# Ten small GpSimd transfers in place of four for each of four x loads: which engine writes which SBUF rows at a time

## The chip, the cores and the metric

The kernel runs on one core of one Trainium2 chip. The metric is the device time of one execution in microseconds, the median of several runs. Before the change it is 1314.01 us (three runs, 1313.97 to 1316.09). Next to the compute engines (TensorE, here PE; VectorE, here DVE; ScalarE, here ACT; GpSimd, here POOL; SyncE, here SP) the core has sixteen DMA engines, numbered 0 to 15, that move data between HBM and SBUF. "Engine 4" and the like always means a DMA engine below.

## The reference

The input is `r_inputs` of shape (4096, 32, 64), 32 fields of 64 float32 numbers for each of 4096 batch rows. For every pair of fields i < j, 496 pairs in all, there is a 64 x 64 weight matrix. What is computed:

```python
i_idx, j_idx = np.triu_indices(32, k=1)
vi = inputs[:, i_idx, :]
vj = inputs[:, j_idx, :]
vdotw = jnp.einsum('bpd,pde->bpe', vi, W)
inter = vdotw * vj
return inter.reshape(B, -1)
```

So each pair's result is a product of a 64-vector with the pair's matrix, multiplied element by element with the other field. The output has 4096 x 496 x 64 float32 numbers, 520 MB, and the inputs are 42 MB: the work is mostly writing.

## The kernel before

**Tiles.** The batch is cut into eight chunks of 512 rows (`BANK`). Two fields make a field pair and fill the 128 partitions, so one chunk of x is 16 tiles of 128 x 512; all 16 lie in one SBUF tensor `x` that is not doubled. All weights stay in SBUF (`w`). A chunk is worked through in 128 steps: for each group of four field pairs (`GROUP`), first a step for the pairs among themselves (L208, L228), then steps of one pair against another (L218, L236). PE writes the products into a ring of eight PSUM banks, and DVE multiplies them with x and writes the result into a slot.

**Slots and stores.** Three slots of 20, 18 and 18 blocks form a ring. When a slot is full, SP issues one store of 4.6 or 5.1 MB (L180), and DVE may write the slot again when that store has landed. Stores are on SP's DMA queue (q1 in the profile).

**x loads.** The next chunk's x comes in two loads: groups 0 and 1 when the current chunk is done with group 1 (L249 to L251), groups 2 and 3 at the chunk's end. Most are one transfer of 128 rows of 16 KB from ACT (L140; q10), eight rows on each DMA engine. The first load of chunks 1, 3, 5 and 7 (`LIGHT_CHUNKS`) is different: it leaves engine 4 out, and goes from GpSimd's queue (L99; q0).

**How engines are chosen.** [...] `from_engine(e)` (L101) issues a "nudge", a transfer of a few bytes on k engines into an otherwise unused tile, so that the next transfer starts at engine e. `load_beside` (L113) then issues, before the change, two transfers for a load: the last eight rows, four each on two engines (from `PAIRS_FROM`: 7 and 8, 15 and 0, 1 and 2, 7 and 8), and rows 0 to 119, eight each on engines 5 to 15 and 0 to 3. With the nudges these are four transfers per load. `kernel` (L273 to L281) lays the rows out in HBM so that each engine reads one stretch, with a pad of 16 numbers between stretches.

**Order.** Instructions stay in program order on each engine. GpSimd's x transfers wait for the PE and DVE instructions that read the old x (an old x is read by PE as moving operand and by DVE as second factor). [...]

Of the kernel before, what the change touches and what calls it, by code (L numbers as in the profile page):

```python
# [8 lines left out]
F32 = mybir.dt.float32  # L9
ALU = mybir.AluOpType  # L10

P = 128
# [7 lines left out]
DMA_ENGINES = 16  # L20
LIGHT = 4
LIGHT_CHUNKS = [1, 3, 5, 7]
PAIRS_FROM = [7, 15, 1, 7]
HEAD = P // DMA_ENGINES
REST = HEAD // 2
PAD = 16


# [33 lines left out]
def is_light(load):  # L62

    return load[1] == 0 and load[0] in LIGHT_CHUNKS


def load_size(load):

    pads = (DMA_ENGINES + 1) * PAD if is_light(load) else 0
    return P * (load[2] - load[1]) * GROUP * BANK + pads  # L70


# [1 line left out]
def pair_bilinear_kernel(  # L74
# [16 lines left out]
    const = ctx.enter_context(tc.tile_pool(name="const", bufs=1))  # L91
    psum = ctx.enter_context(tc.tile_pool(name="ps", bufs=1, space=bass.MemoryType.PSUM))

    nudges = [const.tile([DMA_ENGINES, 16], F32, tag=f"nudge{i}", name=f"nudge{i}") for i in range(2)]
    cursor = 0

    def from_pool(out, in_):

        tc.keep_in_program_order(nc.gpsimd.dma_start(out=out, in_=in_))  # L99

    def from_engine(e):  # L101

        nonlocal cursor
        k = (e - cursor) % DMA_ENGINES
        if k:
            nudge = nudges[e == LIGHT + 1]
            from_pool(
                nudge[:k].rearrange("p (h c) -> p h c", h=2)[:, :, :4],
                x[: k * 8].rearrange("(p h c) -> p h c", p=k, h=2),
            )  # L110
        cursor = e

    def load_beside(at, xt, n_row, lap):  # L113

        nonlocal cursor
        most = DMA_ENGINES - 1
        for e, k, rows, p in (
            (PAIRS_FROM[lap], 2, REST, most * HEAD),
            (LIGHT + 1, most, HEAD, 0),
        ):  # L120
            from_engine(e)
            n = rows * n_row
            lines = x[at : at + k * (n + PAD)].rearrange("(k c) -> k c", k=k)
            from_pool(xt[p : p + k * rows], lines[:, :n])
            at += k * (n + PAD)
            cursor = (e + k) % DMA_ENGINES
# [4 lines left out]
    def load_x(load):  # L131

        at = sum(load_size(before) for before in loads[: loads.index(load)])
        c, g0, g1 = load
        n = (g1 - g0) * GROUP * BANK
        xt = xbuf[:, g0 * GROUP * BANK : g0 * GROUP * BANK + n]
        if is_light(load):
            load_beside(at, xt, n, LIGHT_CHUNKS.index(c))
        else:
            nc.scalar.dma_start(out=xt, in_=x[at : at + P * n].rearrange("(p c) -> p c", p=P))  # L140

    for load in loads:
        if load[0] == 0:
            load_x(load)
# [42 lines left out]
    for c in range(NC):  # L187
        todo = list(enumerate(steps))
        while todo:
            if made == base + room:  # L190
                turn += 1
                base, room = made, SLOTS[turn % len(SLOTS)]
                tag = f"slot{turn % len(SLOTS)}"
                osb = ring.tile([P, room * BANK], F32, tag=tag, name=tag)
            (s, (p, q)), rest = todo[0], todo[1:]
            n = 1
# [28 lines left out]
            if q is None:  # L225
                for h in range(2):
                    rows = slice(h * D, (h + 1) * D)
# [21 lines left out]
            for load in loads:  # L249
                if last and load[0] == c + 1 and load[2] == p // GROUP + 1:  # L250
                    load_x(load)  # L251
# [58 lines left out]
```

## Time and profile before

| What | Value |
|---|---|
| median of the runs | 1314.01 us |
| profiled execution, its own time | 1313.63 us |
| its span | 1311.8 us |
| moved by DMA | 562.39 MB, 429 GB/s on the mean |
| PE, DVE, POOL busy | 81%, 88%, 1% |
| DVE waits for a slot's store | 77.9 us in 48 waits |
| stores, issue to landing (4.6 MB) | 23.6 us, 68 of them |
| x load from ACT, issue to landing | 20.9 us |
| large part of an x load from GpSimd, issue to landing | 31.3 us |

The span is the time from the first to the last instruction on the core; 1.8 us of the profiled execution lie around it. "Issue to landing" runs from the instruction that issues a transfer to the event that tells of its end, and so includes the time that its packets stand in a queue. The share of a DMA queue is the time of its packets as a part of sixteen engines' span.

### The profile page before, as it was taken

The numbers are of one execution on the slowest core, as the hardware profiler recorded it, in microseconds if no ns is written. First come the engines' busy times: TensorE is split into PE (matmuls) and PEld (weight loads), VectorE is DVE, ScalarE is ACT, GpSimd is POOL, SyncE is SP. The second block draws the span as 40 slices with busy tenths as digits, with TensorE's granted clock in tenths as the row PEclk, the third lists the DMA queues.
The fourth block names the chain that finished last, engine by engine and source line by source line (L and its number), as shares of the span: only waits on it lengthen the run. The fifth ranks groups of instructions, "written<-read, shape, count | busy, mean of one in ns | idle before, by whom it ended". The sixth has DMA issues, their size and how long they took to land.

```text
span 1311.8 us, 9391 instructions
## 1 busy us (share of the span) xinstructions
PE 1058.4 (81%) x4096; PEld 401.8 (31%) x4096; DVE 1153.6 (88%) x725; POOL 9.4 (1%) x20
## 2 busy tenths in 40 slices
PE   6888788988778878888788887888777798878882
PEld 2333233333323323333333332323222333233230
DVE  6998789998899879998889998899888998889893
POOL 0000000000000000000000000000000000000000
PEclk9999899998999989999999999899999999999996
DMA  9999999999999999999999999999999999999998
GB/s 390 429 438 432 422 436 431 432 432 433 432 434 429 434 430 432 431 433 430 436 426 437 434 425 423 434 434 435 431 428 435 428 432 429 427 431 437 434 430 363
DMA packets 19625, 562.39 MB, mean 429 GB/s; under 512 B 2688, under 2 KB 2688, under 8 KB 2816
## 3 DMA queue, kind: packets, MB, share of 16 engines
q1 hardware_dynamic: 16560, 528.23, 93.6%
q10 hardware_dynamic: 1872, 25.17, 4.5%
q0 software_dynamic: 1152, 8.39, 1.6%
q8 instruction: 32, 0.52, 0.1%
q14 instruction: 9, 0.07, 0.0%
HBM read 41.68 MB, written 520.09 MB: 428 GB/s over the span
## 4 chain that ended last, share of the span: by engine, by line
DMA 52%; DVE 38%; PE 6%; issue 2%; DVEq 0%
DMA out_dram<-slot 51%; DVE slot L236 34%; PE pring L218 6%; DVE slot L228 3%; PE pring L208 1%; DMA x<-in_x_dram 1%; DVEq L236 0%; DVEq L298 0%; DVEq L228 0%
## 5 line engine op out<-in xcount | busy, mean ns | idle before, releaser
L236 DVE TENSOR_TENSOR slot<-pring,x 128x1024 f32<-128x1024 f32 (+1 forms) x661 | 1078.2, 1699 | 123.3 <-DMA out_dram<-slot 77.9
L218 PE MATMUL pring<-x,w 64*128 64x512 f32 x3840 | 996.3, 628 | 213.1 <-DVE slot L236 202.2
L218 PEld LDWEIGHTS pring<-x,w 64*128 64x128 f32 x3840 | 386.1, 192 | 824.1 <-DVE slot L236 506.3
L228 DVE TENSOR_TENSOR slot<-pring,x 64x1024 f32<-64x1024 f32 x64 | 77.9, 1217 | 13.7 <-PE pring L208 13.2
L208 PE MATMUL pring<-x,w 64*64 64x512 f32 x256 | 65.4, 631 | 16.6 <-DVE slot L236 8.7
L208 PEld LDWEIGHTS pring<-x,w 64*64 64x64 f32 x256 | 15.7, 137 | 61.3 <-DVE slot L236 28.1
L99 POOL DMA_DIRECT2D x<-in_x_dram x8 | 4.7, 588 | 1078.6 <-DVE slot L236 955.8
L99 POOL DMA_DIRECT2D nudge<-in_x_dram x8 | 4.6, 571 | 0.9 <-POOLq L294 0.9
L294 POOL MEMSET const-bfloat16-1.0<- 128x1 bf16 x1 | 0.1, 102 | 0.0
L294 POOL MEMSET const-float32-0.0<- 128x1 f32 x1 | 0.1, 99 | 0.2 <-issue 0.2
L294 POOL MEMSET const-float32-1.0<- 128x1 f32 x1 | 0.1, 99 | 0.0
L294 POOL MEMSET const-uint8-127<- 128x1 uint8 x1 | 0.1, 99 | 0.0
## 6 DMA issues: line engine op xcount, KB each, us to landing
out_dram<-slot SPq DMA_DIRECT2D x68, 4608.0 KB, 23.6
out_dram<-slot SPq DMA_DIRECT2D x35, 5120.0 KB, 22.6
x<-in_x_dram ACTq DMA_DIRECT2D x11, 2048.0 KB, 20.9
out_dram<-slot SPq DMA_DIRECT2D x4, 2560.0 KB, 21.4
x<-in_x_dram POOLq DMA_DIRECT2D x4, 1920.0 KB, 31.3
out_dram<-slot SPq DMA_DIRECT2D x2, 2048.0 KB, 22.4
w<-in_w_dram SPq DMA_DIRECT2D x1, 2816.0 KB, 30.8
x<-in_x_dram ACTq DMA_DIRECT2D x2, 1024.0 KB, 9.5
```

The lines of the kernel that those rows point to most:

```text
L99: tc.keep_in_program_order(nc.gpsimd.dma_start(out=out, in_=in_))
L208: nc.tensor.matmul(pm[o * D : (o + 1) * D, ts(k, BANK)], w_sb[m * D : (m + 1) * D, s * P + k * D : s * P + (k + 1) * D], x_of(pair, m), st ...
L218: nc.tensor.matmul(pm[:, ts(2 * i + k, BANK)], w_sb[m * D : (m + 1) * D, ts(s + i, P)], x_of(p, m), start=True, stop=True,)
L228: nc.vector.tensor_tensor(strided(osb[rows, a : a + BANK], [BANK, 2]), strided(pm[rows, :BANK], [BANK, 2]), strided(x_of(p + 1 - h, h), [2 ...
L236: nc.vector.tensor_tensor(strided(osb[:, a : a + BANK], *blocks_of), strided(pm[:, :BANK], *blocks_of), strided(x_of(q), [BANK, n], [0, 2] ...
L294: nc = bacc.Bacc("TRN2", target_bir_lowering=False, num_devices=1)
```

## The change

`load_beside` now issues six x transfers for a load, each with its first engine, its number of engines and its first row in `LIGHT_PARTS`: one row each on engines 15, 0, 1 and 2 (rows 28 to 31), two rows each on 7 and 8 (rows 60 to 63), four each on 5 to 11 (rows 0 to 27), four each on 12 to 15 and 0 to 3 (rows 64 to 95), and then four each again on both groups (rows 32 to 59 and 96 to 127). Four nudges per load keep the cursor in step, three within the load and one ahead of it, so that there are ten transfers. Between the fourth and the fifth part the cursor has to move by one engine only; that nudge has 3 x 2 x 4 elements on the SBUF side and 2 x 3 x 4 on the HBM side[...]. The nudges use four small tiles in turn. The layout of x in HBM follows. The ACT loads, the stores and all compute stay as they are.

```diff
-PAIRS_FROM = [7, 15, 1, 7]
-HEAD = P // DMA_ENGINES
-REST = HEAD // 2
+QUAD = 4
+LIGHT_PARTS = [(15, 4, 28), (7, 2, 60), (5, 7, 0), (12, 8, 64), (5, 7, 32), (12, 8, 96)]
...
     def from_engine(e):
 
-        nonlocal cursor
+        nonlocal cursor, turns
         k = (e - cursor) % DMA_ENGINES
-        if k:
-            nudge = nudges[e == LIGHT + 1]
+        nudge = nudges[turns % len(nudges)]
+        if k == 1:
+            from_pool(
+                nudge[:3].rearrange("p (h c) -> p h c", h=2)[:, :, :4],
+                x[:64].rearrange("(g r c) -> g r c", g=2, r=4)[:, :3, :4],
+            )
+        elif k:
             from_pool(
                 nudge[:k].rearrange("p (h c) -> p h c", h=2)[:, :, :4],
                 x[: k * 8].rearrange("(p h c) -> p h c", p=k, h=2),
             )
+        turns += k > 0
         cursor = e
 
-    def load_beside(at, xt, n_row, lap):
+    def load_beside(at, xt, n_row):
 
         nonlocal cursor
-        most = DMA_ENGINES - 1
-        for e, k, rows, p in (
-            (PAIRS_FROM[lap], 2, REST, most * HEAD),
-            (LIGHT + 1, most, HEAD, 0),
-        ):
+        for e, k, p in LIGHT_PARTS:
             from_engine(e)
+            rows = QUAD if k > QUAD else QUAD // k
             n = rows * n_row
             lines = x[at : at + k * (n + PAD)].rearrange("(k c) -> k c", k=k)
             from_pool(xt[p : p + k * rows], lines[:, :n])
             at += k * (n + PAD)
             cursor = (e + k) % DMA_ENGINES
```

More of the change, by code (lines that the diff above doesn't have):

```diff
@@ L67, in load_size @@
 def load_size(load):
-    pads = (DMA_ENGINES + 1) * PAD if is_light(load) else 0
+    pads = sum(k for _, k, _ in LIGHT_PARTS) * PAD if is_light(load) else 0
     return P * (load[2] - load[1]) * GROUP * BANK + pads
@@ L92, in pair_bilinear_kernel @@
     psum = ctx.enter_context(tc.tile_pool(name="ps", bufs=1, space=bass.MemoryType.PSUM))
-    nudges = [const.tile([DMA_ENGINES, 16], F32, tag=f"nudge{i}", name=f"nudge{i}") for i in range(2)]
-    cursor = 0
+    nudges = [const.tile([DMA_ENGINES, 16], F32, tag=f"nudge{i}", name=f"nudge{i}") for i in range(4)]
+    cursor = turns = 0
     def from_pool(out, in_):
@@ L137, in load_x @@
         if is_light(load):
-            load_beside(at, xt, n, LIGHT_CHUNKS.index(c))
+            load_beside(at, xt, n)
         else:
@@ L275 @@
         if is_light(load):
-            k = (DMA_ENGINES - 1) * HEAD
-            for part in (rows[k:].reshape(2, -1), rows[:k].reshape(DMA_ENGINES - 1, -1)):
+            for _, k, p in LIGHT_PARTS:
+                part = rows[p : p + (QUAD * k if k > QUAD else QUAD)].reshape(k, -1)
                 x.append(np.pad(part, ((0, 0), (0, PAD))).ravel())
```

## The prediction

> **What bounds the kernel now.** I read the strip of slices first, then the queues, the chain that ended last, the stretches around the x loads, and at last the single packets.
>
> ```profile
> PE   6888788988778878888788887888777798878882
> DVE  6998789998899879998889998899888998889893
> DMA  9999999999999999999999999999999999999998
> q1 hardware_dynamic: 16560, 528.23, 93.6%
> q10 hardware_dynamic: 1872, 25.17, 4.5%
> q0 software_dynamic: 1152, 8.39, 1.6%
> DMA 52%; DVE 38%; PE 6%; issue 2%; DVEq 0%
> ```
>
> The DMA row never falls below 9 before the tail, and the queues' shares (93.6, 4.5, 1.6) sum to 99.7% of sixteen engines: the kernel is the DMA's own time. The chain alternates stores and VectorE because the store ring holds three slots. VectorE is 88% busy, so it has room to catch up.
>
> ```profile
> 125.00:165.00 40.00, 33.02 (x120) 11.81 (x119) 33.39 (x22) 2.04 (x4) 0.91 1.00 424
> 285.00:325.00 40.00, 33.69 (x116) 12.92 (x114) 33.03 (x24) 0.00 (x0) 0.91 1.00 431
> ```
>
> These are stretches of 40 us, with GB/s last. Around the four loads from GpSimd (those I call light) I find 424, 432, 425 and 429; around the same loads from ACT 431, 432 and 433. So all that the light loads lose against plain ones is about (8+0+7+3)/432 of 40 us = 1.7 us. In the packet records a 16 KB packet takes 611 ns and a 36 KB one 1364; packets longer than their size's median add up, in the four light stretches, to 1.85 us per engine on the mean. [...]
>
> The other thing is how long a light load takes:
>
> ```profile
> x<-in_x_dram ACTq DMA_DIRECT2D x11, 2048.0 KB, 20.9
> x<-in_x_dram POOLq DMA_DIRECT2D x4, 1920.0 KB, 31.3
> 124.80 0.58 POOL L99 DMA_DIRECT2D x<-in_x_dram  x1 [122.77 <-PE pring L218]
> 125.92 0.59 POOL L99 DMA_DIRECT2D x<-in_x_dram  x1
> 167.47 1.93 PE L208 MATMUL pring<-x,w 64*64 64x512 f32 x8
> 169.94 2.46 DVE L228 TENSOR_TENSOR slot<-pring,x 64x1024 f32<-64x1024 f32 x2
> ```
>
> With eight rows on most engines both times, the GpSimd load needs 31.3 us and ACT's 20.9. From the first x issue (124.80) to the landing are 1.1 + 31.3 = 32.4 us: it is there at 157.2, and the chunk's first matmul is at 167.5, 10.3 us later. The other three land at 478.0, 797.1 and 1120.1 for matmuls at 490.5, 808.3 and 1132.2. That cover of 10 to 12 us is what I now spend.
>
> [...] an engine with a full store queue shows one GpSimd packet after each 1.364 us store packet, and a packet of 4 bytes (9 ns) costs a turn as a row of 16 KB does. [...] an engine without rows gets four-byte packets in their place. In the second load, after the transfer of four rows on two engines, the others show five small packets one turn apart, then the nudge's two. So a transfer costs every engine (rows per engine + 1) packets. Per load: 5 (two engines, four rows) + 2 (nudge) + 9 (15 engines, eight rows) + 2 (nudge) = 18; 18 x 4 x 16 = 1152, the queue's count exactly. [...]
>
> **The change, part by part.**
>
> *Rows.* Each engine's sum over four loads is unchanged: engines 7 and 8 had 12, 8, 8, 12 rows and get 10 each time; 15, 0, 1 and 2 get 9 instead of 12 once; engine 4 none. Bytes: zero.
>
> *Ports.* [...] I take half of the 1.85 us as won: -0.9 (0 to -1.85).
>
> *GpSimd's instructions.* 24 more at 0.58 us (24 x 0.58 = 13.9 us) on an engine that is 1% busy. They bring 24 x 2 completion and dummy packets and more; at some 5 ns from start to start that is 15 x 4 x 5 ns = 0.3 us of engine time.
>
> *Completion lanes.* The last x part waits until the first (one row on four engines) has landed, some 9 us after issue. Behind it on GpSimd stands only the next nudge. The engines then still have packets of earlier parts, so this costs nothing; without them it would be 3 to 4 us.
>
> *Turns.* The order up to the last x part is now 1, nudge, 2, nudge, 4, 4, nudge, 4, 4 rows per engine: 2+2+3+2+5+5+2+5+5 = 31 packets instead of 5+2+9 = 16. The mean store turn is (16 x 1.364 + 8 x 1.514)/27 = 1.257 us, since each ninth store packet is a completion of no length. Check on before: 16 x 1.257 + 12 x 0.611 + 4.1 (issue to first packet) + 1 = 32.5, seen 32.4. Fifteen more turns are 18.9 us (20.5 at 1.364; I take 19.7), less two rows of 0.61: +18.5. A light load lands 50.9 us after its first issue.
>
> *Where the stall goes.* Issues at 124.8, 445.3, 764.5 and 1087.5 land at 175.7, 496.2, 815.4 and 1138.4: 8.2, 5.7, 7.1 and 6.2 us after the matmuls that read them ran before. PE waits with all matmuls behind it; VectorE follows. PE then restarts slow: after its wait at launch the same matmuls took
>
> ```profile
> 7.93 3.68 PE L208 MATMUL pring<-x,w 64*64 64x512 f32 x8 [7.93 <-DMA x<-in_x_dram]
> 11.66 2.46 DVE L228 TENSOR_TENSOR slot<-pring,x 64x1024 f32<-64x1024 f32 x2 [11.66 <-PE pring L208]
> ```
>
> 3.68 us, not 1.93. So VectorE is late by 10.0, 7.5, 8.9 and 8.0. The next stores, issued at 181.1, 496.6, 820.1 and 1148.3 before, come at 191.1, 504.1, 829.0 and 1156.3, with packets 1.0 us later: 192.1, 505.1, 830.0, 1157.3. The store ahead of each was finished, on the mean engine, at 190.6, 500.7, 830.3 and 1156.7 (from the records; engines spread 4 to 8 us around it). Engine by engine, counting only those already empty, the mean idle is 1.5 + 4.4 + 0.5 + 0.9 = 7.3 us.
>
> *Sum:* +7.3 + 0.3 - 0.9 = +6.7 on the profiled execution of 1313.63 us (1311.8 span and 1.8 around it), which is 0.4 below the median of 1314.01. On the median: 1320.7. VectorE's 77.9 us of waiting for slots does not have to shrink for this: an engine that stood empty has lost that time.
>
> **Bounds.** Landing 2 us earlier, the same sum gives 3.1 us of idle: 1314.0 + 3.1 - 0.6 = 1316.5. Landing 2 us later, or PE slow for that much longer, nearly every engine is empty in all four places: 14.2 us, 1327.6. From there each microsecond counts four times: 3 us later, 18.2, or 1331.6.
>
> **Rivals.**
>
> *The stores in the queue cover it.* Stores land 23.6 us after issue and take about 11, so some 12 us of work is ahead of each; VectorE late by 7 to 10 leaves 2 to 5. For: in the sum above ten engines are still busy in the third place and five in the fourth. Against: after a light load the queue is at its shortest (496.6 was issued with the mean engine 4 us from empty). 1313.1 to 1316.5.
>
> *The small packets take no turns in the new order* (they merge, or go while the store queue is between packets), the load lands by 160, and only the ports remain: 1314.0 - 0.9 = 1313.1, not slower. It decides where the load lands less than 43 us after issue. Against: the spacing of one turn in the records of before.
>
> *The cursor drifts.* The nudge for one engine (3 by 2 by 4 elements against 2 by 3 by 4) moves it by another count. Then engine 4 gets 4 + 3 x 8 = 28 rows, 17 us, and ends about 13.7 us behind the last: 1334 with the stall. Against: nudges by k were exact in all four laps of before (the engine with 1396 ns store packets has no rows).
>
> *A larger stall.* Each restart also starves the slots after it: 1329 to 1345.
>
> **How the numbers follow.** Landing late with emptied queues, 1316.6 to 1329: 0.66. Covered by queued stores: 0.14. No turns: 0.07. Larger stall: 0.09. Drift: 0.04. A measurement here can tell about 0.2% (2.6 us). The range 1314 to 1331 leaves out the drift, most of the larger stall and some of the two cases without a loss. Faster by over 0.2% would need more than the ports can give: 0.03. Within: 0.19, mostly the covered case. Slower: 0.78. The likeliest's own range is 1316.6 to 1329.
>
> **What would show it.** Right: q0 with 33 x 4 x 16 = 2112 packets and unchanged 8.39 MB; the last x part of a light load landing about 50 us after the first issue; PE L208 waiting for x in four places, 5 to 15 us each; PEclk low just after; a DMA row with dents near 192, 505, 830 and 1157 and VectorE waiting less for slots. Ports right: long packets gone in the light stretches. Wrong: no wait for x (turns), waits for x with the DMA share still 1.00 (cover), or one engine's stores ending far behind (drift).

## The result, and the profile after

The changed kernel takes 1336.02 us (median of five runs, 1331.63 to 1338.23) against 1314.01 (five runs, 1311.45 to 1316.09): a ratio of 1.0163, with a 95% interval of 1.0150 to 1.0176. It is 22.0 us slower; 6.7 were forecast, and the range ended at 1331. The profiled execution takes the median's 1336.02 us, with a span of 1333.9, so 22.1 us more span than before. Of all the executions told of below one ran slow (1631.63 us, of run p2): it counts in p2's median and not in its ratio.

From the page of the changed kernel: the strip (the span in 40 equal slices), the queues, and the chain that ended last.

```profile
PEclk9999969999999987999899997999989999799996
DMA  9999989999999998999999999999999999999998
GB/s 393 435 437 424 426 372 437 423 425 427 436 425 436 425 421 380 437 423 420 431 436 427 433 423 408 395 427 434 418 432 431 433 434 423 412 392 422 439 428 383
q1 hardware_dynamic: 16560, 528.23, 92.8%
q10 hardware_dynamic: 1872, 25.17, 4.4%
q0 software_dynamic: 2112, 8.40, 1.6%
DVE 45%; DMA 41%; PE 8%; issue 4%; POOL 0%; DVEq 0%; POOLq 0%
DVE slot L238 43%; DMA out_dram<-slot 25%; DMA x<-in_x_dram 16%; PE pring L220 7%; DVE slot L230 3%; PE pring L210 1%; POOL x L98 0%; POOL nudge L98 0%; DVEq L300 0%; DVEq L238 0%; POOLq L300 0%; DVEq L230 0%
```

The rate of the kernel before, slice by slice:

```profile
GB/s 390 429 438 432 422 436 431 432 432 433 432 434 429 434 430 432 431 433 430 436 426 437 434 425 423 434 434 435 431 428 435 428 432 429 427 431 437 434 430 363
```

q0 has 2112 packets and 8.40 MB, as worked out. The rate falls to 372, 380, 395 and 392 GB/s in four slices two chunks apart, where it was 431 to 436 before, and the queues' shares now sum to 98.8% instead of 99.7%. The x loads, 1% of the chain before, are 16% of it. (Two lines were added above L208: before's L208, L218, L228 and L236 are L210, L220, L230 and L238 here.)

The chain of waits of the changed kernel, as engine, line, what it waited for, us in total, times, longest:

```profile
DVE slot L230 <- PE pring L210: 66.3, 7, 14.7
PEld pring L210 <- issue: 66.2, 73, 8.4
DVE slot L238 <- DMA out_dram<-slot: 52.6, 32, 5.0
PE pring L210 <- DMA x<-in_x_dram: 38.6, 6, 7.6
POOL x L98 <- DMA x<-in_x_dram: 18.6, 4, 4.9
```

The same waits in the kernel before:

```profile
PE pring L208 <- DMA x<-in_x_dram: 7.9, 1, 7.9
DVE slot L228 <- PE pring L208: 13.2, 2, 11.7
```

PE now waits for x at L210 in four places (six waits: one is the launch, and the fourth place has two); before, the only such wait was the one of 7.9 us at launch. DVE stands behind PE for 66.3 us there instead of 13.2, and its waits for a slot's store fall from 77.9 us to 52.6: it now often comes later than the landing that it waited for.

The first of the four places in the timeline of the changed kernel, GpSimd first and then PE and DVE (start, us, engine, line, operation, idle time ahead of it):

```profile
124.64 0.54 POOL L98 DMA_DIRECT2D x<-in_x_dram  x1 [122.63 <-DVE slot L238]
...
133.86 0.55 POOL L98 DMA_DIRECT2D x<-in_x_dram  x1 [4.62 <-DMA x<-in_x_dram]
```

```profile
169.77 1.93 PE L210 MATMUL pring<-x,w 64*64 64x512 f32 x2 [4.33 <-issue]
178.94 3.67 PE L210 MATMUL pring<-x,w 64*64 64x512 f32 x6 [7.23 <-DMA x<-in_x_dram]
```

```profile
182.65 2.48 DVE L230 TENSOR_TENSOR slot<-pring,x 64x1024 f32<-64x1024 f32 x2 [14.73 <-PE pring L210]
```

Of the eight matmuls that ran at 167.47, two start at 169.77, and the other six wait for x until 178.94, 54.3 us after the first x issue. Those six take 3.67 us, where all eight took 1.93. The same happens at 506.7, 832.3 and 1160.1, which is 53.3, 54.5 and 54.6 us after the first issue. One window of five microseconds behind each of these places (stretch, us, PE, PEld, DVE and POOL busy, PEclk, DMA share, GB/s):

```profile
190.00:195.00 5.00, 4.33 (x20) 1.84 (x19) 4.24 (x3) 0.00 (x0) 1.00 0.10 41
510.00:515.00 5.00, 5.00 (x13) 2.45 (x13) 3.67 (x3) 0.00 (x0) 0.50 0.28 120
840.00:845.00 5.00, 4.58 (x19) 2.02 (x16) 4.05 (x3) 0.00 (x0) 0.99 0.79 342
1175.00:1180.00 5.00, 4.25 (x20) 1.70 (x18) 5.00 (x5) 0.00 (x0) 1.00 0.51 220
```

DMA is down to a tenth in the first. That is the loss in plain sight: the next store is issued at 194.2 (181.1 in the kernel before), and by then every DMA engine has run dry.

The packet records give the sizes. Set one behind the other for each engine, they leave gaps of 13.8 us on the mean engine outside launch and tail (before: 0.0). Packets that take longer than the median of their size ("long packets" below) exceed it by 16.5 us per engine in all (before: 7.1). The mean engine ends 23.9 us later: 13.8 + 9.4 + 0.7. Idle engines were forecast, at 7.3 us. The 9.4 us of longer packets were not, and most of the experiments are about them.

### The profile page after: what moved, and what is told of

It reads as the page before. It is cut to its first block, busy times and chain, and to the rows that moved or that the text cites. A ratio compares the mean times of both kernels' runs of the same rounds, so it can differ in the third digit from the quotient of the medians.

```text
span 1333.9 us, 9432 instructions
## 1 busy us (share of the span) xinstructions
PE 1066.9 (80%) x4096; PEld 404.9 (30%) x4096; DVE 1151.7 (86%) x725; POOL 23.0 (2%) x44
## 3 DMA queue, kind: packets, MB, share of 16 engines
q0 software_dynamic: 2112, 8.40, 1.6%
## 4 chain that ended last, share of the span: by engine, by line
DVE 45%; DMA 41%; PE 8%; issue 4%; POOL 0%; DVEq 0%; POOLq 0%
DVE slot L238 43%; DMA out_dram<-slot 25%; DMA x<-in_x_dram 16%; PE pring L220 7%; DVE slot L230 3%; PE pring L210 1%; POOL x L98 0%; POOL nudge L98 0%; DVEq L300 0%; DVEq L238 0%; POOLq L300 0%; DVEq L230 0%
## 5 line engine op out<-in xcount | busy, mean ns | idle before, releaser
L238 DVE TENSOR_TENSOR slot<-pring,x 128x1024 f32<-128x1024 f32 (+1 forms) x661 | 1075.8, 1697 | 93.0 <-DMA out_dram<-slot 52.6
L220 PE MATMUL pring<-x,w 64*128 64x512 f32 x3840 | 991.1, 628 | 184.9 <-DVE slot L238 175.9
L220 PEld LDWEIGHTS pring<-x,w 64*128 64x128 f32 x3840 | 386.9, 192 | 790.4 <-DVE slot L238 465.7
L230 DVE TENSOR_TENSOR slot<-pring,x 64x1024 f32<-64x1024 f32 x64 | 77.9, 1217 | 66.8 <-PE pring L210 66.3
L210 PE MATMUL pring<-x,w 64*64 64x512 f32 x256 | 79.0, 683 | 57.1 <-DMA x<-in_x_dram 38.6
L210 PEld LDWEIGHTS pring<-x,w 64*64 64x64 f32 x256 | 18.0, 147 | 112.8 <-issue 66.2
L98 POOL DMA_DIRECT2D x<-in_x_dram x24 | 13.3, 562 | 1085.9 <-DVE slot L238 751.0
L98 POOL DMA_DIRECT2D nudge<-in_x_dram x16 | 9.8, 613 | 6.4 <-DMA nudge<-in_x_dram 5.4
## 6 DMA issues: line engine op xcount, KB each, us to landing
out_dram<-slot SPq DMA_DIRECT2D x4, 2560.0 KB, 21.6
```

Source lines behind the costliest of these rows:

```text
L210: nc.tensor.matmul(pm[o * D : (o + 1) * D, ts(k, BANK)], w_sb[m * D : (m + 1) * D, s * P + k * D : s * P + (k + 1) * D], x_of(pair, m), st ...
L220: nc.tensor.matmul(pm[:, ts(2 * i + k, BANK)], w_sb[m * D : (m + 1) * D, ts(s + i, P)], x_of(p, m), start=True, stop=True,)
L230: nc.vector.tensor_tensor(strided(osb[rows, a : a + BANK], [BANK, 2]), strided(pm[rows, :BANK], [BANK, 2]), strided(x_of(p + 1 - h, h), [2 ...
L238: nc.vector.tensor_tensor(strided(osb[:, a : a + BANK], *blocks_of), strided(pm[:, :BANK], *blocks_of), strided(x_of(q), [BANK, n], [0, 2] ...
```

## The experiments

Each kernel is timed against the kernel before, on the same chip. Theory *turns* is the prediction's: every GpSimd transfer puts small packets on every engine, each taking one turn behind a store packet (1.364 us for one of 36 KB, 1.514 for one of 40), so the last row lands late. *Ports* stands for the new split of rows and engines as such; what it would act on, no view shows.

### Turns alone, in two places

**d7** is the kernel before with seven GpSimd transfers of a few bytes, on all sixteen engines, ahead of the large part of each light load; the rows and their engines stay as before.

```diff
+    spare = [const.tile([DMA_ENGINES, 16], F32, tag=f"spare{i}", name=f"spare{i}") for i in range(IDLE)]
...
+    def idle():
+
+        for t in spare:
+            from_pool(
+                t.rearrange("p (h c) -> p h c", h=2)[:, :, :4],
+                x[: DMA_ENGINES * 8].rearrange("(p h c) -> p h c", p=DMA_ENGINES, h=2),
+            )
...
+            if k == most and lap in IDLE_LAPS:
+                idle()
```

> The kernel before, rows and ports untouched, with seven more tiny transfers on all sixteen engines (two packets each, 14 turns) put ahead of the large part of each of the four loads. Turns: the large part lands about 18 us later, 50 us after the first issue; four waits for x of 10 to 15 us; 1330 to 1340 us. Ports (the new split of rows and engines is what costs): 1314 within 3 us, no wait for x. Number of GpSimd transfers: as slow as turns, 1330 or more.

Measured: 1336.21 us, ratio 1.0179 (1.0162 to 1.0196). From d7's chain of waits:

```profile
PE pring L221 <- DMA x<-in_x_dram: 75.4, 5, 18.9
```

Five waits, the launch among them. Without a new row order the whole loss is there, with much the same gaps (14.4 us per engine) and long packets (17.7). So a loss of this size needs no new row order.

**b7** issues the same seven behind the large part, where nothing reads what lands late (`idle()` at the end of `load_beside`).

> The same seven transfers per load, but behind the large part, so that x has no packet behind them. Turns: x lands as before, about 32 us after the first issue, no wait for x, 1314 within 3 us. Number of GpSimd transfers (descriptors, completions, small packets as such): 1330 to 1340, as with them ahead. Ports: 1314.

Measured: 1324.41 us, ratio 1.0091 (1.0074 to 1.0108). PE waits for x only at launch (7.7 us), the engines' gaps are 0.4 us, as turns says; yet it is 12 us slower, where turns said nothing. There are more long packets here too, 14.6 us per engine, those of the ACT loads among them (2.5 us against 0.3), which no GpSimd transfer stands beside. Turns alone fails.

**s26** is the changed kernel with its large parts first and the leftover rows on four and four engines behind them.

```diff
-LIGHT_PARTS = [(15, 4, 28), (7, 2, 60), (5, 7, 0), (12, 8, 64), (5, 7, 32), (12, 8, 96)]
+LIGHT_PARTS = [(5, 7, 0), (12, 8, 64), (5, 7, 32), (12, 8, 96), (4, 4, 28), (8, 4, 60)]
```

> The changed kernel with its four large parts as they are, but first, and the eight rows that are left on engines 4 to 7 and 8 to 11, one each, without nudges of their own: 26 packets per engine to the last row instead of 31, seven x and nudge transfers per load instead of ten. Engine 4 gets one row per load, 5 to 11 nine. Turns: landing about 44 us after the first issue, waits for x of 1 to 5 us that the queued stores mostly cover: 1314 to 1320. Ports: 1330 or more, since the large parts write as in the changed kernel. Number of transfers: half way, about 1323.

Measured: 1324.16 us, ratio 1.0085 (1.0070 to 1.0101); gaps 0.5 us, long packets 15.4 us. Beside the launch PE waits for x four times, 11.1 us in all, and the queued stores cover that, as turns says. The same surplus as in b7 is left.

**d7_first** has d7's seven transfers in the first light load only (`IDLE_LAPS = [0]`).

> As the seven transfers ahead, in the first of the four loads only. Turns: one wait for x near 166 us, DMA empty for 4 to 5 us near 190, nothing at the other three loads: 1318 to 1321. If store packets also get longer because all engines restart together after the empty stretch, packets longer than usual show in the 200 us behind it and not from 600 us on; if they come from the new ports, there are none here.

Measured: 1326.39 us, ratio 1.0110 (1.0089 to 1.0130). Beside the launch there is one wait of PE for x (20.4 us), with gaps of 6.1 us, but also 14.7 us of long packets, 7.0 of them behind 600 us. They follow neither the stall nor the number of transfers: b7, with four times as many extra transfers, has 14.6 us.

### The place of the tiles in SBUF

What these kernels share with the changed one is a detail of the edit that the prediction gave no cost: more 64-byte tiles stand ahead of x in SBUF (the changed kernel's list of nudge tiles has four instead of two), and everything behind them moves. In the kernel before, x starts at byte 16640 of each partition, the slots at 112896, 153856 and 190720, all multiples of 256. Two tiles more make it 128 bytes past such a multiple; seven more (d7, b7, d7_first) 192 bytes past. That a start off a multiple of 256 costs anything was a guess at this point, and nothing had shown it. The next four runs put it to the test: **p2** moves everything in the kernel before by 128 bytes and does nothing else; **after_al**, **b7_al** and **s26_al** ("al" for aligned) are the changed kernel, b7 and s26 moved on to a multiple of 256. Theory A in the expectations says that the place costs, theory B that the extra transfers themselves do. The edit of p2:

```diff
+    for i in range(2):
+        const.tile([DMA_ENGINES, 16], F32, tag=f"room{i}", name=f"room{i}")
     xbuf = const.tile([P, NPR * BANK], F32, tag="x", name="x")
```

> The kernel before with two unused 64-byte tiles allocated ahead of x, nothing else: x, w and the three slots lie 128 bytes further on in every partition (x from byte 16768 instead of 16640, which is 65 x 256), as in the changed kernel. Theory A (place in SBUF: x loads and stores are slower from starts that are no multiple of 256 bytes, and the changed kernel's four 64-byte nudge tiles, the other runs' seven more, put them there): 1321 to 1325, packets longer than their size's median adding up to 12 to 16 us per engine instead of 7. Theory B (the longer packets come from the extra GpSimd transfers themselves): 1313 to 1315, 6 to 8 us.

> The changed kernel with two unused 64-byte tiles more, so that x starts at 16896 = 66 x 256. Theory A: the stall alone is left, 1334 - 8 = 1324 to 1328, with the four waits of PE for x and the four dents as in the changed kernel, and long packets back to 6 to 8 us per engine. Theory B: 1332 to 1338.

> Seven transfers behind the large part as in b7, with one unused 64-byte tile more (ten in all, x at 17152 = 67 x 256). Theory A with the turns: 1313 to 1316, since nothing reads what lands late. Theory B: 1322 to 1326, as b7.

> The changed kernel's large parts first and the leftover rows on four and four engines, as in s26, with x at 16896 = 66 x 256. Theory A: 1312 to 1317, as no load lands late. Theory B: 1322 to 1326, as s26.

| Kernel | us | ratio (95%) | long packets, us per engine | gaps, us per engine |
|---|---|---|---|---|
| p2 | 1322.10 | 1.0054 (1.0036 to 1.0073) | 13.9 | 0.1 |
| after_al | 1331.83 | 1.0130 (1.0114 to 1.0145) | 11.0 | 15.1 |
| b7_al | 1316.60 | 1.0018 (1.0011 to 1.0024) | 8.8 | 0.2 |
| s26_al | 1319.07 | 1.0034 (1.0022 to 1.0046) | 9.7 | 0.3 |

Two unused tiles cost 7 us, and in the other three two or one more unused tiles take 4 to 8 us off. So the place costs, with and without extra transfers, and theory B, which gave p2 no loss, falls as the account of the long packets. Theory A's numbers were too low for three kernels all the same: after_al keeps 17 us where 10 to 14 were expected (taken alone it is nearer to theory B's 1332), so the stall is larger than forecast, and b7_al and s26_al keep some 2 and 5 where 0 to 2 and -2 to 3 were.

Next: is it the place or the move, and what reads or writes there? **p4** has four unused tiles (256 bytes), **p12** twelve (all starts at multiples of 1024). **x_off** shifts x by 128 bytes and brings w and the slots back to a multiple of 256; **slots_off** shifts the slots alone.

```diff
     xbuf = const.tile([P, NPR * BANK], F32, tag="x", name="x")
...
         done += n
 
+    for i in range(2):
+        const.tile([DMA_ENGINES, 16], F32, tag=f"room{i}", name=f"room{i}")
     pring = psum.tile([P, BANKS * BANK], F32, tag="pring", name="pring")
```

(slots_off; x_off has two such tiles ahead of x and two ahead of w.)

> The kernel before with four unused 64-byte tiles ahead of x: everything 256 bytes further on, x at 16896 = 66 x 256. Theory A (starts that are no multiple of 256 bytes cost): 1313 to 1315, long packets 6 to 8 us per engine. Rival (any move away from the old place costs, or the unused tiles do): 1320 to 1323, as with two tiles.

> The kernel before with twelve unused 64-byte tiles ahead of x, so that x, w and the slots all start at multiples of 1024 bytes (x at 17408 = 17 x 1024; before 16640 = 65 x 256). If 256 bytes is all that counts: 1313 to 1315. If larger powers count too: 1307 to 1312, long packets below 6 us per engine.

> x alone off by 128 bytes: two unused tiles ahead of x and two between x and w, so that w and the slots lie at multiples of 256 (+256 bytes) and x does not. If it is what the x loads write that costs: 1320 to 1323, as with everything moved by 128. If it is what the stores read: 1313 to 1315. Both: 1316 to 1319.

> The slots alone off by 128 bytes: two unused tiles between w and the first slot, x and w where they were. If it is what the stores read that costs: 1320 to 1323. If it is what the x loads write: 1313 to 1315. Both: 1316 to 1319.

| Kernel | us | ratio (95%) | long packets, us per engine |
|---|---|---|---|
| p4, all +256 | 1314.22 | 1.0003 (0.9994 to 1.0011) | 7.6 |
| p12, all at 1024 | 1314.29 | 1.0001 (0.9993 to 1.0010) | 6.3 |
| x_off, x +128 | 1314.41 | 0.9999 (0.9990 to 1.0008) | 8.0 |
| slots_off, slots +128 | 1322.95 | 1.0061 (1.0040 to 1.0081) | 13.2 |

It is the place of the slots alone, which the stores read (1.0061); where the x loads write does not matter (0.9999), and multiples of 1024 win nothing over 256 (1.0001). VectorE writes the slots too, but its instructions (L236 of the kernel before) take 1699 ns on the mean in both kernels. The stretch of 40 us around the ACT load of the second half of chunk 3, for the kernel before, x_off and slots_off in turn:

```profile
480.00:520.00 40.00, 32.76 (x116) 12.31 (x116) 35.34 (x24) 0.00 (x0) 0.91 1.01 432
```

```profile
480.00:520.00 40.00, 32.34 (x116) 12.15 (x116) 34.03 (x23) 0.00 (x0) 0.91 1.00 429
```

```profile
480.00:520.00 40.00, 32.89 (x114) 12.43 (x116) 34.04 (x23) 0.00 (x0) 0.87 1.01 419
```

The DMA share is full in all three (1.01, 1.00 and 1.01), but 13 GB/s are gone in the last. Not every packet pays: by the packet records the median 36 KB packet takes 1364 ns in all of them. A few packets take very long instead: 129 of 8704 over 1.2 times that median in slots_off, 43 before and 49 in x_off. They gather where x loads run beside the stores: 104 of the 129 start within 2.5 us of a row of an x load, as only a fifth of all 36 KB packets do. In stretches with stores alone slots_off has 435 and 432 GB/s (45 to 85 and 205 to 245 us), the kernel before 434 and 433.

### How many turns fit, and what they cost with aligned slots

The 17 us that after_al keeps are more than the forecast. **d3_al**, **d5_al** and **d7_al** put three, five and seven transfers ahead of the large part, with aligned slots. **p1** shifts everything by 64 bytes.

> The kernel before with three transfers of one small row per engine ahead of the large part of each light load, slots at multiples of 256 bytes: 6 packets more ahead of the last row, 6 x 1.31 = 7.9 us, landing 40.3 us after the first issue, still inside the cover of 10.3 to 12.4 us. Turns with cover: no wait of PE for x but the one at launch, 1313 to 1317. If extra transfers cost by themselves (8.5 us over seven in a light load's worth, no threshold): 1319 to 1322.

> Five such transfers: 10 packets more, 13.1 us, landing 45.5 us after the first issue, 0.7 to 2.8 us past the cover. Turns with cover: short waits of PE for x, stores late by 2 to 4 us into queues that hold 5 to 9 us, so 1314 to 1320. Proportional without a threshold: 1324 to 1327.

> Seven such transfers, as in d7, with the slots at multiples of 256 bytes: 14 packets more ahead of the last row, landing about 52 us after the first issue. Turns are the whole of what is left: 1328 to 1333, idle 13 to 16 us per engine, as the changed kernel with aligned slots (1331.8). The new rows and the last part's wait have a share: 1322 to 1327.

> The kernel before with one unused 64-byte tile ahead of x: the slots at 64 past a multiple of 256 bytes. If every start off 256 costs alike: 1320 to 1324. If only the half (128) matters, or the cost grows with the offset: 1313 to 1318.

| Kernel | us | ratio (95%) | first x issue to the first matmul behind it, four places | gaps, us per engine |
|---|---|---|---|---|
| d3_al | 1315.77 | 1.0017 (1.0010 to 1.0024) | 39.6 (the one with a wait) | 0.0 |
| d5_al | 1315.95 | 1.0018 (1.0010 to 1.0025) | 44.3, 44.2, 44.9, 48.5 | 0.0 |
| d7_al | 1328.05 | 1.0106 (1.0086 to 1.0126) | 52.5, 54.4, 52.4, 53.5 | 7.8 |
| p1 | 1322.22 | 1.0068 (1.0048 to 1.0087) | as before | 0.3 |

d5_al shows the cover at work. Its strip and its waits for x:

```profile
DMA  9999999999999999999999999999999999999998
```

```profile
PE pring L223 <- DMA x<-in_x_dram: 34.5, 5, 8.7
```

PE waits 5 to 9 us in all four places, restarts slowly, and no engine goes idle: the stores in the queue hold that long. Two transfers more, and it is over. d7_al's strip and rates:

```profile
DMA  9999999999999998999999999999999999999998
GB/s 390 436 432 431 424 425 434 431 429 434 430 432 433 430 420 382 426 425 429 429 440 429 436 429 414 425 429 428 432 432 423 441 425 436 408 404 426 439 429 375
```

Of its gaps, 4.2 and 2.4 us lie in the second and the fourth place (the slices with 382 and 404 GB/s), 0.3 and 0.9 in the other two. So the cost is no line through zero but has a threshold: up to 45 to 48 us from the first issue it is 2 us, at 52 to 54 us 14. How it grows beyond, no run shows.

There is a rival for the threshold: in d7_al GpSimd stands 8.9 to 10.2 us ahead of the seventh extra transfer until x of the first part has landed, and then waits once more, and so it issues the large part only 16 to 17 us after the first x issue. In d5_al it does so 3.6 us after it. The packet records speak against it. In d7_al GpSimd's packets go on without a break until the last rows, never more than 0.8 us apart among the engines and about one per engine and turn: so small ones were still standing in the queues when the large part came. d7_al (11.3 to 16.5 us by its interval) and after_al (15.0 to 19.1) overlap, so the new rows and their engines add between nothing and a few microseconds; they save nothing that shows. d7_al's profile is of its fastest run (1325.03, the others 1328.0 to 1328.9), so its 7.8 us of gaps, where 13 to 16 were expected, are on the low side.

In p1 a start 64 bytes off costs as much as 128 (1.0068; p2 1.0054, slots_off 1.0061).

## Why the prediction was right in its direction and wrong in its size

*Rows, 0.* Right: 8.40 MB on q0.

*Turns.* Right in kind, and too small. The turn of 1.257 us stands on the records of the kernel before: on an engine eight store packets are mostly followed by one of 4 bytes and 9 ns. q0 has the 2112 packets worked out, and d7_al, with the rows of the kernel before and aligned slots, makes waits and gaps in the same four places from turns alone. The landing comes 53.3 to 54.6 us after the first issue, not 50.9; with aligned slots 51.4, 53.8, 54.1 and 53.6. That is as if each of the fifteen turns cost 1.35 to 1.53 us with aligned slots (landing less 32.4, and 1.2 back for the two rows), where 1.31 had been taken. For six more packets the same sum (40.3) met 39.6, for ten (45.5) 44.2 to 48.5. Why a turn gets dearer is open. That the last part's wait (*Completion lanes*) stays hidden fits: in the first load GpSimd waited 4.6 us until the first part had landed and issued the last part 9.2 us after the first, and its packets go on without a break meanwhile. No run took the wait away alone.

*Where the stall goes.* The mechanism is right: four waits of PE, a restart of 3.67 us (3.68 forecast), late stores, dents at 190 to 195, 510 to 515, 840 to 845 and 1175 to 1180 us. The size is not: 7.3 us of idle time were forecast, 13.8 were measured, and 15.1 in after_al. In the first place after_al is nearly as forecast (store issued at 190.2 for 191.1; 0.9 us idle for 1.5), the other three take 7.6, 3.4 and 3.2 us for 4.4, 0.5 and 0.9. In those three the landing is 2.7 to 3.2 us later than the 50.9, and the prediction's own bounds give 14.2 us of idle time for 2 us of delay and 18.2 for 3. These bounds were lopsided (2 us earlier, 3.1 us of idle time), so an error of 3 us in the landing was enough: 50.9 lies between the landings of d5_al, which cost nothing of this kind, and those of d7_al.

*The steps that failed* are two. The larger is the term "Where the stall goes": +7.3 for 13.8 to 15.1, mis-sized through the landing. The other isn't in the list at all. The change part by part goes through rows, ports, instructions, lanes, turns; the two additional nudge tiles, 128 bytes, were put at nothing without a word. They moved the slots off a multiple of 256. With aligned slots the changed kernel is 4.2 us faster (1336.02 and 1331.83; ratios of 1.0163 and 1.0130 whose intervals don't meet), and its long packets fall from 16.5 to 11.0 us. Without this the kernel would have stood just past the range's end, not 5 us beyond it, and still at well over twice the loss that was forecast.

*Ports, -0.9.* Not seen, and the mechanism was not shown: the -0.9 is the author's estimate, half of the 1.85 us of long packets in the four light stretches. In after_al the long packets of the light loads themselves fall from 0.64 to 0.37 us per engine, but those of the stores rise by 4.1, and in d7_al, with the old rows, by 3.7. So that rise needs no new rows.

*GpSimd's instructions, +0.3.* Too small: b7_al, d3_al and d5_al, whose extra transfers delay nothing that stops the DMA, are 2.2 to 2.4 us slower by their ratios. It is not in proportion (28, 12 and 20 transfers), and their long packets (8.8, 9.3 and 8.2 us, before 7.1) go with it. s26_al, with twelve transfers more and the new rows, is 4.5 us slower (2.9 to 6.0). Why is open.

| Term | forecast, us | shown, us |
|---|---|---|
| idle engines after late landings | +7.3 | +15.1 (after_al) |
| place of the slots | none | +4.2 (after and after_al) |
| more GpSimd transfers | +0.3 | +2.3 (b7_al, d3_al, d5_al) |
| ports | -0.9 | not seen |
| sum | +6.7 | +21.6, of 22.0 measured |

The right column puts together numbers of several kernels, and a profile is of one execution; that it comes so close to 22.0 is in part luck.

*The rivals.* Stores in the queue cover it: its mechanism exists (d5_al), but it doesn't reach as far as this change's landing. No turns: falls, by d7 and the packet count. Drift: falls, since all engines run dry together (DMA share 0.10 at 190 to 195 us). `cursor` is the code's own count, and the packet records give no engine numbers; in the second light load of the kernel before they show eight rows on thirteen engines, twelve on two and none on one, as the code intends. A larger stall, 1329 to 1345 at 0.09, holds the time, though not by its mechanism: the engines' gaps lie in the four places alone, and nothing behind them starves.

**What stays open.** Why a store that reads from a start off a multiple of 256 bytes makes a few packets very long beside x loads, and leaves the rest alone. Why the same landing leaves 7.8 us of gaps in one profile (d7_al) and 15.1 in another (after_al). And why extra transfers that delay nothing cost some 2 us.

## What to carry to other kernels

Before costing an edit's instructions, ask what its new tiles move: here 128 bytes of scratch ahead of the big buffers cost 7 to 9 us in the kernel before and 4 in the changed one, and moving the buffers that the stores read on to a multiple of 256 bytes took that back (p4 1.0003, after_al 4.2 us). Count a GpSimd transfer by the packets it puts on every engine's queue, each a turn behind a store packet (1.35 to 1.53 us here), and put small transfers behind the one that somebody waits for. When a forecast rests on a cover of a few microseconds, look for the threshold: at it, waits of 5 to 9 us on PE cost next to nothing, and landing some 8 us later cost 12 us more.

## What the runs showed of the hardware that was not expected

- Stores of 36 and 40 KB packets from SBUF at 64 or 128 bytes past a multiple of 256 make this kernel 0.5 to 0.7% slower (p1, p2, slots_off: 1.0068, 1.0054, 1.0061). For x loads that write to such a place the ratio is 0.9999 (0.9990 to 1.0008). Starts at multiples of 1024 give 1.0001.
- The loss is in few packets: 1.2 to 1.5% of the 36 KB store packets take over 1.2 times the median of 1364 ns in these three runs, 0.5% in the kernel before. The longest take 2.6 us, and 2.5 before. They come mostly while x loads are in flight (104 of 129 in slots_off within 2.5 us of a row of x), and some packets of those loads are long too: the ACT loads' add 1.2 us per engine in slots_off and 0.3 before.
- PE restarts slowly after a wait of 5 us as after one of 19: the eight matmuls of before's L208 take 3.4 to 3.7 us in d5_al, d7_al and d7 alike. In d3_al they take 1.93 after a wait of 1.3 us, as without a wait, and 2.69 after one of 3.3 us for VectorE.
